# New orders for every engine's queue in a token-block and convolution kernel, and one more square on VectorE

## The chip, the core and the metric

The kernel runs on one core of a Trainium2 chip. The metric is the device time of one execution in microseconds (us), as the median of several runs. A core has five engines that work side by side, each with its own queue, in order: TensorE (PE: matrix products and transposes, results in PSUM; PEld is its weight load), VectorE (DVE), ScalarE (ACT), GpSimd (POOL), and SyncE (SP), which here issues DMAs. An instruction waits, at the head of its engine's queue, for semaphores of the engines whose results or buffers it needs; what stands behind it waits too.

## The reference

Input x is (4, 128, 128, 128) in float32: four images, 128 channels, 128 x 128 pixels. Two layers follow each other, each on a group-normalised input and added to it:

```python
# layer 0, for each token (pixel) t of 128 channels; it is applied to the image and to
# its transpose and added: for a token-wise block that is twice the same
t = _ln(t, ln0_g, ln0_b)
y1 = _ln(t, ln1_g, ln1_b)
t = t + einsum('btc,oc->bto', sigmoid(y1) * y1, W_out)
y2 = _ln(t, ln2_g, ln2_b)
wht = einsum('btc,oc->bto', y2, W_whiten)
k = square(relu(einsum('btc,hc->bth', wht, W_key)))        # 512 wide
kv = einsum('bth,ch->btc', k, W_value)
r = sigmoid(einsum('btc,oc->bto', wht, W_recep))
t = t + r * kv
...
x = x + _L0_conv_ref(_gn(x), ...)
x = x + _L1_conv_ref(_gn(x), ...)   # 3 x 3 convolution, bias, times a squeeze-and-excite gate
```

## The kernel before

**Tiling.** Tokens go in 64 pairs, 16 to an image; a pair is two halves of 512 tokens, each of four 128-token pieces. In an operation's name the first digit after the letters is the half or the norm's number, a second digit is the half or the key block; the number after the colon says which pair or convolution block is meant, relative to the slot, or counted from somewhere, according to the list. The convolution works on 32 blocks of 16 rows (8 to an image), where each group of four output rows comes from six products (c0 to c5) in place of twelve, after Winograd; each product is three matrix products (L875 to L877) of shifted columns. Its inputs v0 to v5 and outputs y0 to y3 are sums on VectorE.

**One token pair, in order of data.** ACT lays the group norm on the input (u), TensorE transposes it (Tu, L659), VectorE takes statistics (bn, L690), POOL makes the norm's factors (nb, L707 to L725, with the power at L718; in the first two pairs VectorE does the rest and POOL the power, names sa and pw), ACT applies it (t, L666), POOL multiplies and shifts (g at L742, b at L746). Then the second norm (bn1, nb1, ACT's z, L666), a transpose (Tz), ACT's silu (L757), TensorE's product (att, L763), VectorE's sum (T, L767), the third statistics (bn2, nb2). The third norm's factors go through HBM to be spread over the partitions: VectorE turns them (rc, L775), SP writes four short rows (W, L781) and reads them back as R (L786, twice 256 KB), while TensorE transposes t (tt). VectorE multiplies the two (cp, L799). From that come four key products for each half (pk, L810), ACT's relu (re, L814), the square (sq, on ACT at L820, or on VectorE at L824, where it reads pk again), the gate's product (pr, L828) with ACT's tanh (th, L832), four value products that add up in one bank (kv, L837), and VectorE's and POOL's sums back into the block (S L847, q L853, x L857), whose statistics (bx, L863) the second layer's norm uses. Around this, fetch and in0/in1 (L998, L1004) read the next image and take its statistics.

**Order.** A manual schedule: every engine runs its instructions in the order in which the lists name them. FILL (L37) starts pairs 0 to 5 and the first slots; FIRST (L66) is repeated for slots 6 to 16, where no convolution is there yet; HANDOVER (L80) leads to the second image, with the setup of the first image's convolution; ORDER (L25) is repeated for 21 slots (23 to 30, 39 to 46, 55 to 59), each with a token pair at several ages and half a convolution block; BOUND (L143) leads twice from one image to the next; END (L210) has the last four pairs and all the convolution of the last image. In these, `*` is the next step of a convolution's setup (statistics mv, pm, pv, root rs, scaled weights, gate; L555 to L632), `+` one of the next image's input norm, `load` reads a block. After the last token pairs, END is convolution alone.

**Buffers.** PSUM's eight banks: two for ut, two for the transposes and att (tr), two for keys (h), one for the convolution and one for kv. Until pair 18 every third key product goes to the convolution's bank (key_bank, L801). A bank comes free when its last reader ends. In SBUF there are six relu outputs h, two u, two z, four t, three R and two r.

**Squares.** FIRST_SQUARES (L270) says for the pairs of the first image which key blocks of each half are squared on ACT (A) or VectorE (D); SQUARES has A everywhere for the other three images.

Of the kernel before, what the change touches and what calls it, by code (L numbers as in the profile page):

```python
# [25 lines left out]
    u1:0 Tu1:0 u0:0 x11:3 Tz10:1 Tu0:0 bn01:0 bn00:0 z11:1 bx1:3 v1:1 pr0:2 Tz11:1 q2:1  # L26
    silu0:1 p2:1 re00:2 sq00:2 y2:1 ca:1 att0:1 silu1:1 c0:1 pk01:2 nb0:0 d8:1 kv00:2 T0:1
    y0:1 th0:2 t1:0 bn20:1 v3:1 tt1:2 g1:0 re01:2 in0:0 c1:1 cp1:2 e1:1 att1:1 pk02:2 c3:1
    T1:1 bn21:1 pk10:2 c5:1 b1:0 y3:1 re02:2 S1:2 t0:0 nb2:1 e3:1 pk03:2 v2:1 g0:0 b0:0
    re10:2 c2:1 in1:0 a:1 pk12:2 sq01:2 sq10:2 v0a:1 sq02:2 re03:2 sq03:2 re12:2 b:1 kv01:2  # L30
    kv02:2 rc:1 pk13:2 re13:2 v4:1 pk11:2 kv03:2 sq12:2 c4:0 bn11:0 v5a:0 tt0:1 bn10:0 v0b:1
    pr1:2 q0:2 c:0 d:0 re11:2 sq11:2 S0:1 sq13:2 kv10:2 v5b:0 kv11:2 th1:2 kv12:2 kv13:2
    nb1:0 W:1 y1:0 R0:1 z10:0 q:0 cp0:1 pk00:1 R1:1 x10:2 p:0 bx0:2 q1:2
# [4 lines left out]
    fetch:16 u1:0 u0:0 Tu1:0 bn01:0 u0:1 Tu0:0 u1:1 bn00:0 sa0:0 in1:16 pw0:0 in0:16  # L38
    fetch:17 nb0:0 t1:0 t0:0 Tu0:1 g1:0 bn00:1 b1:0 u1:2 Tu1:1 in1:17 g0:0 u0:2 in0:17
    bn11:0 fetch:18 b0:0 bn01:1 sa0:1 bn10:0 pw0:1 sa1:0 nb0:1 pw1:0 in1:18 t0:1 in0:18  # L40
    nb1:0 fetch:19 t1:1 Tu1:2 g0:1 bn01:2 b0:1 z10:0 Tu0:2 bn00:2 g1:1 z11:0 Tz10:0 b1:1
    in0:19 silu0:0 Tz11:0 bn10:1 nb0:2 u0:3 att0:0 in1:19 silu1:0 bn11:1 fetch:20 u1:3
    att1:0 sa1:1 T0:0 bn20:0 pw1:1 t0:2 T1:0 t1:2 bn21:0 g0:2 sa2:0 Tu0:3 nb1:1 pw2:0 Tu1:3
    in1:20 u1:4 in0:20 z10:1 g1:2 bn00:3 fetch:21 z11:1 bn01:3 nb2:0 b0:2 Tz10:1 rc:0 nb0:3
    W:0 silu0:1 Tz11:1 att0:1 silu1:1 in1:21 bn10:2 R0:0 att1:1 in0:21 b1:2 t0:3 T0:1
    fetch:22 T1:1 tt0:0 t1:3 g0:3 bn11:2 R1:0 tt1:0 Tu1:4 nb1:2 cp0:0 u0:4 bn20:1 u0:5 Tu0:4
    pk02:0 in1:22 S1:0 u1:5 bn01:4 pk00:0 re02:0 pk01:0 re00:0 g1:3 cp1:0 pk03:0 z10:2
    sq00:0 b1:3 bn00:4 pk11:0 re01:0 b0:3 re03:0 pr0:0 in0:22 z11:2 bn21:1 fetch:23 kv00:0
    nb0:4 pk10:0 S0:0 sq01:0 bn10:3 Tz10:2 re11:0 kv01:0 silu0:2 sa2:1 pk12:0 re10:0 bn11:3
    att0:2 sq02:0 pw2:1 sq03:0 kv02:0 T0:2 th0:0 nb2:1 nb1:3 Tz11:2 t1:4 rc:1 kv03:0 sq10:0  # L50
    W:1 pk13:0 q0:0 silu1:2 Tu1:5 in0:23 re12:0 att1:2 bn20:2 t0:4 R0:1 pr1:0 g1:4 bn01:5
    kv10:0 sq11:0 R1:1 x10:0 T1:2 Tu0:5 sq12:0 kv11:0 z10:3 bn00:5 tt1:1 tt0:1 nb0:5 kv12:0
    th1:0 cp0:1 re13:0 pr0:1 sq13:0 cp1:1 pk03:1 z11:3 S1:1 pk00:1 bn21:2 th0:1 kv13:0 g0:4
    S0:1 re00:1 Tz11:3 bx0:0 pk01:1 re03:1 b1:4 sq00:1 silu1:3 pk02:1 b0:4 bn11:4 re01:1
    Tz10:3 att1:3 re02:1 nb2:2 bn10:4 silu0:3 pk12:1 q1:0 pk10:1 re12:1 T1:3 att0:3 sq03:1
    bn21:3 sq01:1 kv00:1 nb1:4 re10:1 pk11:1 sq02:1 rc:2 sq10:1 W:2 pk13:1 re11:1 T0:3
    kv01:1 sq11:1 bn20:3 t1:5 kv02:1 x11:0 R0:2 kv03:1 sq12:1 nb2:3 tt0:2 q0:1 re13:1 R1:2
    pr1:1 bx1:0 t0:5 kv10:1 S0:2 kv11:1 sq13:1 kv12:1 x10:1 z10:4 cp0:2 tt1:2 pk01:2 g0:5
    S1:2 th1:1 pk00:2 cp1:2 re01:2 g1:5 pk03:2 re00:2 rc:3 kv13:1 sq00:2 re03:2 in1:23
    pk02:2 q1:1 pk10:2 bx0:1 x11:1 kv00:2 Tz10:4 bx1:1  # L60
# [6 lines left out]
    u1:0 u0:0 Tu1:0 pk11:4 re02:4 pr0:4 z11:2 Tu0:0 in1:0 re10:4 silu0:2 Tz11:2 sq01:4  # L67
    bn01:0 W:3 att0:2 b1:1 sq10:4 bn00:0 R0:3 T0:2 th0:4 silu1:2 re11:4 kv01:4 b0:1 pk12:4
    sq03:4 tt0:3 bn10:1 sq02:4 pk13:4 sq11:4 cp0:3 re12:4 pr1:4 att1:2 th1:4 kv02:4 re13:4
    kv03:4 nb0:0 bn11:1 bn20:2 T1:2 S0:3 pk01:3 pk00:3 pk03:3 bn21:2 tt1:3 t0:0 q0:4 kv10:4  # L70
    nb1:1 sq12:4 kv11:4 re01:3 re00:3 sq13:4 in0:0 nb2:2 S1:3 kv12:4 sq00:3 kv13:4 R1:3
    x10:4 cp1:3 pk02:3 rc:2 q1:4 bx0:4 t1:0 x11:4 g1:0 z10:1 bx1:4 pk10:3 kv00:3 Tz10:1 g0:0
    re03:3
# [7 lines left out]
    load load load fetch:32 sq01:13 W:14 z11:15 re02:13 Tz11:15 R0:14 silu0:15 kv01:13 u1:17  # L81
    att0:15 R1:14 silu1:15 b0:16 pk11:13 T0:15 re10:13 att1:15 bn20:15 b1:16 u0:17 pk13:13
    re11:13 T1:15 Tu1:17 * bn21:15 tt0:14 re13:13 pr1:13 sq03:13 sq10:13 nb2:15 pr0:13
    sq02:13 bn01:17 u1:18 Tu0:17 pk12:13 bn00:17 sq11:13 kv02:13 th0:13 bn10:16 nb0:17
    sq13:13 tt1:14 kv03:13 th1:13 cp0:14 re12:13 q0:13 pk00:14 u0:18 bn11:16 kv10:13 sq12:13
    re00:14 pk01:14 cp1:14 x10:13 t1:17 S1:14 kv11:13 sq00:14 pk03:14 nb1:16 S0:14 t0:17
    Tu1:18 kv12:13 re01:14 pk12:14 bn01:18 re03:14 Tu0:18 u0:19 pk02:14 bn00:18 g0:17
    kv13:13 z10:16 rc:15 W:15 g1:17 tt0:15 q1:13 pk10:14 sq03:14 S0:15 sq01:14 nb0:18
    kv00:14 * re12:14 kv01:14 * re02:14 R0:15 * re10:14 pr0:14 bx0:13 sq02:14 R1:15 sq10:14
    pk11:14 sq12:14 Tz10:16 th0:14 b0:17 kv02:14 t1:18 kv03:14 x11:13 cp0:15 pk13:14 re11:14  # L90
    bn10:17 b1:17 t0:18 pk00:15 q0:14 pr1:14 bn11:17 sq11:14 x10:14 Tu0:19 * tt1:15 kv10:14
    * * nb1:17 th1:14 * kv11:14 re00:15 * kv12:14 cp1:15 re13:14 bn00:19 silu0:16 pk02:15
    sq13:14 sq00:15 re02:15 kv13:14 g0:18 S1:15 u1:19 pr1:15 q1:14 z11:16 b0:18 att0:16
    bx0:14 pk01:15 x11:14 z10:17 Tu1:19 Tz11:16 g1:18 bn01:19 pk03:15 th1:15 silu1:16
    kv00:15 T0:16 nb0:19 re01:15 bn20:16 pr0:15 z11:17 att1:16 bn10:18 re03:15 in1:32
    Tz11:17 pk10:15 sq01:15 T1:16 b1:18 sq03:15 bn21:16 Tz10:17 kv01:15 re10:15 nb2:16
    sq02:15 sq10:15 pk11:15 silu1:17 bx1:14 kv02:15 th0:15 kv03:15 silu0:17 t0:19 q0:15
    att0:17 rc:16 x10:15 bn11:18 W:16 pk12:15 re11:15 bx1:13 tt0:16 nb1:18 sq11:15 pk13:15
    T0:17 u0:20 bx0:15 t1:19 R0:16 Tu0:20 bn20:17 kv10:15 kv11:15 R1:16 re12:15 S0:16
    re13:15 att1:17 bn00:20 g0:19 sq12:15 sq13:15 kv12:15 g1:19 * kv13:15 cp0:16 u1:20 *  # L100
    b1:19 u1:21 Tu1:20 q1:15 pk01:16 z10:18 bn01:20 x11:15 pk00:16 nb0:20 re01:16 bx1:15
    Tz10:18 pr0:16 re00:16 T1:17 sq00:16 * tt1:16 silu0:18 bn21:17 * th0:16 att0:18 sq01:16
# [164 lines left out]
"""  # L267

SQUARES = ("AAAA", "AAAA")
FIRST_SQUARES = ("DAAA", "DAAA")  # L270

ON_GPSIMD = set()
END_ON_GPSIMD = {"p2", "q2"}
# [912 lines left out]
```

## Time and profile before

| what | us |
|---|---|
| median of three runs (1869.79 to 1872.17) | 1870.11 |
| the profiled execution | 1872.87 |
| its span in the profile | 1871.1 |
| TensorE busy | 1806.3 |
| VectorE busy | 1348.0 |
| ACT busy | 1269.8 |
| POOL busy | 1164.7 |
| ACT's squares (L820), 480 | 286.5 |
| VectorE's squares (L824), 32 | 23.6 |

The profiled execution took 1.8 us more than its span, and 2.8 us more than the median of the runs. A page has one line for every group of instructions: its line in the code, engine, operation, what it writes and reads, number, then busy time and mean duration in ns, then the time that the engine stood idle before them, with what ended it. In a timeline, a line gives start, duration and the instruction, and in brackets the idle time before it. One record of TensorE may last beyond the start of the next, since products are pipelined.

### The profile page before, as it was taken

Reading aid. Unit: us, or ns where it says so; the run is one execution under the profiler, and the core shown is the slowest. Engines: PE = TensorE matmul, PEld = TensorE weight load, DVE = VectorE, ACT = ScalarE, POOL = GpSimd, SP = SyncE. Lnnn points to the kernel's source line nnn. Section 1 sums busy time; section 2 is a strip of 40 time slices with the busy share of each in tenths; the row PEclk is TensorE's granted clock in tenths of the full one; section 3 lists DMA queues with packets and bytes.
Section 4 is the critical chain, followed back from the end, with each engine's and each line's share of the span. In section 5 each row is a group of like instructions: output and inputs, shape, how many; then the busy total and the mean of one; then the engine's idle time right before and its main releaser. Section 6 shows DMA issues by size and latency. Waiting matters only on the chain.

```text
span 1871.1 us, 21825 instructions
## 1 busy us (share of the span) xinstructions
PE 1806.3 (97%) x6096; PEld 942.6 (50%) x6096; DVE 1348.0 (72%) x3336; ACT 1269.8 (68%) x2493; POOL 1164.7 (62%) x1915
## 2 busy tenths in 40 slices
PE   3799999999999999999999999999999999999999
PEld 2555555555545555455455455455455555554443
DVE  6767766677677677777757677777766667676987
ACT  2889899898666776777667777677766777753000
POOL 2878888887366666886556666788555667641211
PEclk9899999999999999999999999999999999999999
DMA  5211112221212212222112212211201111111112
GB/s 219 89 46 57 46 49 96 73 71 58 71 59 85 91 68 103 84 87 96 42 68 91 77 50 77 75 63 68 81 12 68 68 57 68 50 39 45 52 68 90
DMA packets 46072, 133.57 MB, mean 71 GB/s; under 512 B 8679, under 2 KB 15102, under 8 KB 38014
## 3 DMA queue, kind: packets, MB, share of 16 engines
q1 hardware_dynamic: 45504, 131.77, 20.5%
q8 instruction: 49, 0.80, 0.2%
q14 instruction: 73, 0.60, 0.1%
q10 hardware_dynamic: 446, 0.40, 0.1%
HBM read 97.14 MB, written 35.00 MB: 71 GB/s over the span
## 4 chain that ended last, share of the span: by engine, by line
PE 84%; DVE 5%; POOL 5%; DMA 3%; ACT 2%; issue 1%; SPq 0%; DVEq 0%; POOLq 0%
PE kv L837 21%; PE pk L810 21%; PE m L875 8%; PE m L877 8%; PE m L876 8%; PE pr L828 5%; PE att L763 5%; PE tt L659 3%; PE ut L659 3%; PE z1t L659 3%; DMA x<-in_x 1%; POOL rs L718 1%; DMA R<-rd 1%; DVE st L690 1%; ACT t L666 1%
## 5 line engine op out<-in xcount | busy, mean ns | idle before, releaser
L810 PE MATMUL pk<-y,wk_s 128*128 128x512 f32 x1024 | 503.3, 594 | 1.6 <-ACT h L814 0.9
L837 PE MATMUL kv<-h,wv 128*128 128x512 f32 x1024 | 492.7, 593 | 0.0
L814 ACT ACTIVATE h<-pk,kbias 128x512 f32<-128x512 f32 x512 | 349.3, 687 | 188.1 <-PE pk L810 178.3
L857 POOL TENSOR_TENSOR x<-x,r 128x512 f32<-128x512 f32 x128 | 166.7, 1302 | 202.4 <-DVE r L853 193.2
L837 PEld LDWEIGHTS kv<-h,wv 128*128 128x128 f32 x1024 | 187.1, 190 | 201.9 <-issue 177.2
L820 ACT ACTIVATE h<-h 128x512 f32<-128x512 f32 x480 | 286.5, 629 | 3.4
L810 PEld LDWEIGHTS pk<-y,wk_s 128*128 128x128 f32 x1024 | 183.0, 191 | 185.2 <-issue 148.0
L666 ACT ACTIVATE t<-ut,nb,rs 128x128 f32<-128x128 f32 x512 | 191.4, 466 | 90.6 <-POOL nb L725 82.7
L690 DVE BATCH_NORM_STATS2 st<-t 128x6 f32<-128x128 f32 x1024 | 219.0, 278 | 30.5 <-POOL t L746 28.7
L666 ACT ACTIVATE z<-t,nb,rs 128x128 f32<-128x128 f32 x512 | 209.5, 489 | 17.5 <-POOL nb L725 17.1
L718 POOL TENSOR_TENSOR rs<-rs,nhalf 128x8 f32<-128x8 f32 x128 | 215.4, 1682 | 6.0 <-DVE rs L711 6.0
L742 POOL TENSOR_TENSOR t<-t,g 128x512 f32<-128x512 f32 x128 | 163.8, 1285 | 74.7 <-ACT t L666 74.3
L875 PE MATMUL m<-v,u 128*128 128x512 f32 x384 | 198.5, 598 | 10.4 <-DVE v L899 5.0
L877 PE MATMUL m<-v,u 128*128 128x508 f32 x384 | 195.7, 591 | 0.0
L876 PE MATMUL m<-v,u 128*128 128x508 f32 x384 | 195.5, 591 | 0.0
L746 POOL TENSOR_TENSOR t<-t,b 128x512 f32<-128x512 f32 x128 | 166.0, 1304 | 5.6
L853 DVE SCALAR_TENSOR_TENSOR r<-r,kv 128x512 f32<-128x512 f32 x128 | 87.0, 680 | 86.2 <-PE kv L837 83.4
L763 PEld LDWEIGHTS att<-wo,y 128*128 128x128 f32 x1024 | 131.9, 196 | 31.5 <-issue 22.4
L767 DVE TENSOR_TENSOR t<-att,t 128x512 f32<-128x512 f32 x128 | 87.7, 685 | 78.3 <-PE att L763 77.8
L690 DVE BATCH_NORM_STATS2 st<-ut 128x6 f32<-128x128 f32 x512 | 112.3, 283 | 40.4 <-PE ut L659 39.8
L763 PE MATMUL att<-wo,y 128*128 128x128 f32 x1024 | 138.0, 280 | 0.8 <-DVE t L767 0.4
L828 PE MATMUL pr<-y,wr_s 128*128 128x512 f32 x256 | 130.7, 594 | 0.9 <-DVE h L824 0.7
(164 smaller groups left out, 2491.2 us busy)
## 6 DMA issues: line engine op xcount, KB each, us to landing
R<-rd SPq DMA_DIRECT2D x128, 256.0 KB
x<-in_x SPq DMA_DIRECT2D x31, 1024.0 KB
out<-x SPq DMA_DIRECT2D x31, 1024.0 KB
xs<-in_x SPq DMA_DIRECT2D x48, 512.0 KB
rd<-rrow SPq DMA_DIRECT2D x256, 1.0 KB
u<-raw SPq DMA_DIRECT2D x18, 192.0 KB
raw<-u SPq DMA_DIRECT2D x6, 192.0 KB
x<-in_x SPq DMA_DIRECT2D x2, 512.0 KB
```

The costliest lines, as they stand in the source:

```text
L666: nc.scalar.activation(dst[:, s, :], src[:, s, :], AF.Identity, bias=nb[:, i : i + 1], scale=rs[:, i : i + 1],)
L690: nc.vector.bn_stats(st[:, h * SUB + s, :], src[:, s, :])
L718: nc.gpsimd.tensor_tensor(rs, rs, nhalf, ALU.pow)
L763: nc.tensor.matmul(att[:, ts(s, P)], y[:, ts(s, P)], wo, start=True, stop=True)
L810: nc.tensor.matmul(pk, wk_s[:, ts(j, P)], S["y2", g, h], start=True, stop=True)
L814: nc.scalar.activation(k, S["pk", g, h, j], AF.Relu, bias=kbias[:, j : j + 1])
L820: nc.scalar.activation(k, k, AF.Square)
L828: nc.tensor.matmul(pr, wr_s, S["y2", g, h], start=True, stop=True)
L837: nc.tensor.matmul(S["kv", g, h], wv[:, j, :], S.pop(("h", g, h, j)), start=(j == 0), stop=(j == NH - 1))
L875: nc.tensor.matmul(pc, u[:, 1], v, start=True, stop=False)
L876: nc.tensor.matmul(pc[:, :, 1:W], u[:, 0], v[:, :, 0 : W - 1], start=False, stop=False)
L877: nc.tensor.matmul(pc[:, :, 0 : W - 1], u[:, 2], v[:, :, 1:W], start=False, stop=True)
```

## The change

All six lists are replaced. Each new list has the same operations as the old one, so that no operation is added or taken away; what changes is the order on each engine's queue, among them the loads and the writes and reads of R on SP's. How the new lists were made isn't in the code. The functions stay as they are, and so do the numbers of slots. In FIRST_SQUARES one more letter is D: in the 16 pairs of the first image, the second key block of the second half (sq11) is squared on VectorE. The heads of the long lists are shown, ORDER and FIRST whole:

```diff
--- before.py
+++ after.py
 ORDER = """
-    u1:0 Tu1:0 u0:0 x11:3 Tz10:1 Tu0:0 bn01:0 bn00:0 z11:1 bx1:3 v1:1 pr0:2 Tz11:1 q2:1
-    silu0:1 p2:1 re00:2 sq00:2 y2:1 ca:1 att0:1 silu1:1 c0:1 pk01:2 nb0:0 d8:1 kv00:2 T0:1
-    y0:1 th0:2 t1:0 bn20:1 v3:1 tt1:2 g1:0 re01:2 in0:0 c1:1 cp1:2 e1:1 att1:1 pk02:2 c3:1
-    T1:1 bn21:1 pk10:2 c5:1 b1:0 y3:1 re02:2 S1:2 t0:0 nb2:1 e3:1 pk03:2 v2:1 g0:0 b0:0
-    re10:2 c2:1 in1:0 a:1 pk12:2 sq01:2 sq10:2 v0a:1 sq02:2 re03:2 sq03:2 re12:2 b:1 kv01:2
-    kv02:2 rc:1 pk13:2 re13:2 v4:1 pk11:2 kv03:2 sq12:2 c4:0 bn11:0 v5a:0 tt0:1 bn10:0 v0b:1
-    pr1:2 q0:2 c:0 d:0 re11:2 sq11:2 S0:1 sq13:2 kv10:2 v5b:0 kv11:2 th1:2 kv12:2 kv13:2
-    nb1:0 W:1 y1:0 R0:1 z10:0 q:0 cp0:1 pk00:1 R1:1 x10:2 p:0 bx0:2 q1:2
+    u1:0 p:1 kv00:3 u0:0 z10:1 sq02:3 Tu0:0 kv01:3 Tu1:0 kv02:3 re03:3 d:1 bn00:0 rc:2
+    Tz10:1 bn01:0 c2:2 in1:0 re12:3 z11:1 pk11:3 nb0:0 sq03:3 Tz11:1 a:2 silu0:1 sq10:3 W:2
+    sq12:3 re11:3 kv03:3 silu1:1 t0:0 R0:2 sq11:3 q2:1 q:1 tt0:2 t1:0 pk13:3 pr1:3 v3:1 c3:1
+    q0:3 re13:3 th1:3 att1:1 v4:1 b:2 g0:0 v1:1 e3:1 v5a:0 kv10:3 S0:2 cp0:2 att0:1 b0:0
+    g1:0 kv11:3 sq13:3 b1:0 T1:1 pk02:2 T0:1 y1:1 re02:2 y2:1 ca:1 kv12:3 bn10:0 bn11:0
+    v5b:0 x10:3 pk01:2 R1:2 bn20:1 re01:2 kv13:3 tt1:2 pr0:2 v0a:1 cp1:2 nb1:0 c0:1 sq01:2
+    v0b:1 q1:3 y0:1 th0:2 c1:1 pk00:2 bn21:1 pk10:2 bx0:3 x11:3 c5:1 e1:1 d8:1 re00:2 sq00:2
+    bx1:3 re10:2 in0:0 c4:0 pk12:2 c:0 nb2:1 y3:1 S1:2 p2:0 pk03:2 v2:1
 """
 
 
...
 FILL = """
-    fetch:16 u1:0 u0:0 Tu1:0 bn01:0 u0:1 Tu0:0 u1:1 bn00:0 sa0:0 in1:16 pw0:0 in0:16
-    fetch:17 nb0:0 t1:0 t0:0 Tu0:1 g1:0 bn00:1 b1:0 u1:2 Tu1:1 in1:17 g0:0 u0:2 in0:17
-    bn11:0 fetch:18 b0:0 bn01:1 sa0:1 bn10:0 pw0:1 sa1:0 nb0:1 pw1:0 in1:18 t0:1 in0:18
-    nb1:0 fetch:19 t1:1 Tu1:2 g0:1 bn01:2 b0:1 z10:0 Tu0:2 bn00:2 g1:1 z11:0 Tz10:0 b1:1
-    in0:19 silu0:0 Tz11:0 bn10:1 nb0:2 u0:3 att0:0 in1:19 silu1:0 bn11:1 fetch:20 u1:3
-    att1:0 sa1:1 T0:0 bn20:0 pw1:1 t0:2 T1:0 t1:2 bn21:0 g0:2 sa2:0 Tu0:3 nb1:1 pw2:0 Tu1:3
-    in1:20 u1:4 in0:20 z10:1 g1:2 bn00:3 fetch:21 z11:1 bn01:3 nb2:0 b0:2 Tz10:1 rc:0 nb0:3
-    W:0 silu0:1 Tz11:1 att0:1 silu1:1 in1:21 bn10:2 R0:0 att1:1 in0:21 b1:2 t0:3 T0:1
-    fetch:22 T1:1 tt0:0 t1:3 g0:3 bn11:2 R1:0 tt1:0 Tu1:4 nb1:2 cp0:0 u0:4 bn20:1 u0:5 Tu0:4
-    pk02:0 in1:22 S1:0 u1:5 bn01:4 pk00:0 re02:0 pk01:0 re00:0 g1:3 cp1:0 pk03:0 z10:2
-    sq00:0 b1:3 bn00:4 pk11:0 re01:0 b0:3 re03:0 pr0:0 in0:22 z11:2 bn21:1 fetch:23 kv00:0
-    nb0:4 pk10:0 S0:0 sq01:0 bn10:3 Tz10:2 re11:0 kv01:0 silu0:2 sa2:1 pk12:0 re10:0 bn11:3
...
+    fetch:16 u0:0 u1:0 Tu0:0 bn00:0 u0:1 Tu1:0 u1:1 bn01:0 sa0:0 in0:16 pw0:0 in1:16
+    fetch:17 nb0:0 t0:0 t1:0 Tu0:1 g0:0 bn00:1 u1:2 Tu1:1 g1:0 in0:17 u0:2 b1:0 bn01:1
+    in1:17 b0:0 bn11:0 fetch:18 sa0:1 bn10:0 pw0:1 sa1:0 nb0:1 pw1:0 in1:18 t0:1 in0:18
+    fetch:19 nb1:0 t1:1 Tu1:2 g0:1 bn01:2 b0:1 z10:0 Tu0:2 g1:1 bn10:1 z11:0 Tz10:0 bn00:2
+    b1:1 silu0:0 Tz11:0 bn11:1 att0:0 silu1:0 sa1:1 u1:3 att1:0 in0:19 u0:3 pw1:1 in1:19
+    T0:0 fetch:20 nb0:2 nb1:1 T1:0 z11:1 bn20:0 Tz11:1 bn21:0 silu1:1 sa2:0 t1:2 att1:1
+    in0:20 pw2:0 in1:20 t0:2 fetch:21 Tu1:3 g1:2 T1:1 bn01:3 u1:4 Tu0:3 g0:2 z10:1 bn00:3
+    nb2:0 b1:2 rc:0 Tz10:1 W:0 b0:2 bn11:2 silu0:1 bn21:1 nb0:3 u0:4 att0:1 bn10:2 R0:0
+    tt0:0 in1:21 R1:0 in0:21 T0:1 nb1:2 t1:3 S0:0 fetch:22 tt1:0 bn20:1 t0:3 Tu1:4 cp0:0
+    sa2:1 pk01:0 u1:5 S1:0 g0:3 z11:2 cp1:0 pk00:0 bn01:4 b0:3 pk03:0 re00:0 in1:22 Tz11:2
+    re01:0 g1:3 Tu0:4 sq00:0 silu1:2 pk10:0 bn00:4 pw2:1 z10:2 att1:2 bn10:3 kv00:0 re03:0
+    b1:3 T1:2 Tz10:2 sq01:0 pr0:0 bn21:2 re10:0 nb0:4 pk02:0 silu0:2 bn11:3 kv01:0 re02:0
...
 FIRST = """
-    u1:0 u0:0 Tu1:0 pk11:4 re02:4 pr0:4 z11:2 Tu0:0 in1:0 re10:4 silu0:2 Tz11:2 sq01:4
-    bn01:0 W:3 att0:2 b1:1 sq10:4 bn00:0 R0:3 T0:2 th0:4 silu1:2 re11:4 kv01:4 b0:1 pk12:4
-    sq03:4 tt0:3 bn10:1 sq02:4 pk13:4 sq11:4 cp0:3 re12:4 pr1:4 att1:2 th1:4 kv02:4 re13:4
-    kv03:4 nb0:0 bn11:1 bn20:2 T1:2 S0:3 pk01:3 pk00:3 pk03:3 bn21:2 tt1:3 t0:0 q0:4 kv10:4
-    nb1:1 sq12:4 kv11:4 re01:3 re00:3 sq13:4 in0:0 nb2:2 S1:3 kv12:4 sq00:3 kv13:4 R1:3
-    x10:4 cp1:3 pk02:3 rc:2 q1:4 bx0:4 t1:0 x11:4 g1:0 z10:1 bx1:4 pk10:3 kv00:3 Tz10:1 g0:0
-    re03:3
+    u0:0 u1:0 re03:4 Tu1:0 bn10:1 th0:4 z11:2 re02:4 R0:3 Tu0:0 kv00:4 pk12:4 bn01:0 silu0:2
+    pk11:4 bn00:0 R1:3 att0:2 in1:0 sq02:4 kv01:4 T0:2 re12:4 re11:4 pk13:4 Tz11:2 sq03:4
+    b1:1 bn11:1 in0:0 sq12:4 nb0:0 pk10:4 sq11:4 tt0:3 kv02:4 re13:4 bn20:2 cp0:3 S0:3
+    silu1:2 kv03:4 pr1:4 re10:4 t1:0 sq13:4 t0:0 tt1:3 th1:4 q0:4 sq10:4 pk01:3 nb1:1 att1:2
+    x10:4 S1:3 pk00:3 re01:3 T1:2 kv10:4 bn21:2 g0:0 kv11:4 sq01:3 kv12:4 bx0:4 re00:3
+    kv13:4 q1:4 sq00:3 nb2:2 x11:4 cp1:3 rc:2 bx1:4 b0:0 pk03:3 z10:1 pr0:3 W:2 pk02:3 g1:0
+    Tz10:1
 """
 FIRST_SLOTS = 17
...
 HANDOVER = """
-    load load load fetch:32 sq01:13 W:14 z11:15 re02:13 Tz11:15 R0:14 silu0:15 kv01:13 u1:17
-    att0:15 R1:14 silu1:15 b0:16 pk11:13 T0:15 re10:13 att1:15 bn20:15 b1:16 u0:17 pk13:13
-    re11:13 T1:15 Tu1:17 * bn21:15 tt0:14 re13:13 pr1:13 sq03:13 sq10:13 nb2:15 pr0:13
...
+    load load load z11:15 u0:17 u1:17 re03:13 Tu1:17 Tz11:15 th0:13 bn01:17 Tu0:17 silu0:15
+    pr1:13 bn00:17 b1:16 sq03:13 att0:15 fetch:32 silu1:15 bn10:16 kv00:13 nb0:17 re02:13
+    R0:14 att1:15 sq02:13 bn11:16 u0:18 pk13:13 R1:14 T1:15 th1:13 pk10:13 bn21:15 re13:13
...
 BOUND = """
-    p2:-3 q2:-3 fetch:0 v3:-3 x11:-4 * u0:-1 u1:-1 load Tu0:-1 z11:-2 Tu1:-1 re00:-3 Tz10:-2
-    pk01:-3 v1:-3 * bn00:-1 bn01:-1 v0a:-3 v4:-3 c3:-3 + * sq00:-3 Tz11:-2 silu0:-2 re01:-3
-    att0:-2 silu1:-2 v2:-3 in0:0 nb0:-1 e3:-3 att1:-2 t0:-1 + T0:-2 g0:-1 c1:-3 + e1:-3
-    tt1:-3 b0:-1 bn20:-2 T1:-2 + cp1:-3 t1:-1 pk03:-3 re03:-3 + in1:0 sq03:-3 bn21:-2
-    bn10:-1 c2:-3 + g1:-1 pk10:-3 + kv00:-3 pk02:-3 u0:0 a:-3 Tu0:0 b1:-1 b:-3 u0:1 p:-2
-    fetch:1 bn11:-1 sq01:-3 v0b:-3 v5a:-3 re02:-3 bn00:0 c4:-3 c:-3 u1:0 re10:-3 Tu1:0
...
+    z10:-2 u0:-1 Tz10:-2 rc:-3 u1:-1 Tu0:-1 kv00:-4 z11:-2 Tu1:-1 q2:-3 Tz11:-2 v3:-3
+    kv01:-4 load silu0:-2 W:-3 bn00:-1 silu1:-2 att0:-2 re03:-4 bn01:-1 p:-3 nb0:-1 re12:-4
+    sq02:-4 + att1:-2 c3:-3 q:-3 sq12:-4 R0:-3 * T0:-2 kv02:-4 T1:-2 sq03:-4 v1:-3 + e3:-3
+    v4:-3 fetch:0 + kv03:-4 pk13:-4 t0:-1 g0:-1 tt0:-3 t1:-1 sq10:-4 q0:-4 re13:-4 + cp0:-3
+    R1:-3 bn21:-2 c1:-3 + pk11:-4 b0:-1 + g1:-1 re11:-4 bn10:-1 bn20:-2 kv10:-4 b1:-1 +
+    in1:0 x10:-4 bn11:-1 tt1:-3 pk00:-3 sq13:-4 S0:-3 in0:0 e1:-3 pr1:-4 nb1:-1 re00:-3
...
 END = """
-    u1:3 Tu1:3 u0:3 d8:-5 z11:4 Tu0:3 bn00:3 Tz10:4 bn01:3 pk03:5 Tz11:4 silu0:4 x11:6
-    re00:5 silu1:4 att0:4 pr0:5 y2:-5 att1:4 re03:5 nb0:3 T0:4 bn20:4 c0:-5 sq00:5 th0:5
-    kv00:5 tt1:5 t0:3 t1:3 pk01:5 T1:4 bn21:4 u1:2 re01:5 nb2:4 ca:-5 sq01:5 g0:3 p:-4 p2:-4
-    y0:-5 cp1:5 pk02:5 u0:2 c5:-5 sq03:5 bx1:6 re02:5 S1:5 g1:3 b1:3 rc:4 y3:-5 b0:3 bn11:3
-    bn10:3 kv01:5 Tu1:2 sq02:5 pk10:5 nb1:3 bn01:2 re10:5 Tu0:2 sq10:5 pk11:5 q:-4 v1:-4 W:4
-    pk13:5 kv02:5 tt0:4 re11:5 pr1:5 re13:5 kv03:5 th1:5 c1:-4 z10:3 bn00:2 z11:3 v2:-4 R0:4
-    Tz10:3 q0:5 cp0:4 q2:-4 pk12:5 silu0:3 nb0:2 pk00:4 re12:5 x10:5 e1:-4 v5a:-4 v3:-4 S0:4
-    R1:4 v0a:-4 t1:2 t0:2 v0b:-4 g1:2 kv10:5 att0:3 Tz11:3 T0:3 pr0:4 g0:2 sq11:5 silu1:3
-    re00:4 load c3:-4 sq13:5 sq12:5 kv11:5 u1:1 att1:3 b0:2 bn10:2 sq00:4 pk02:4 b1:2 kv12:5
-    bn11:2 tt1:4 kv13:5 nb1:2 T1:3 e3:-4 Tu1:1 c2:-4 u0:1 th0:4 re02:4 S1:4 bn21:3 bn20:3
-    u0:0 q1:5 a:-4 z10:2 b:-4 pk01:4 cp1:4 Tu0:1 pk03:4 kv00:4 bx0:5 re01:4 nb2:3 pk10:4
...
+    u1:3 u0:3 Tu1:3 z11:4 kv00:6 Tz11:4 d:-5 re03:6 sq03:6 bn01:3 rc:5 z10:4 Tu0:3 bn00:3
+    nb0:3 silu1:4 c2:-5 sq02:6 re12:6 att1:4 t1:3 kv01:6 Tz10:4 T1:4 t0:3 kv02:6 kv03:6 a:-5
+    b:-5 g0:3 W:5 y2:-5 g1:3 b1:3 y1:-5 ca:-5 pk13:6 R1:5 silu0:4 d8:-5 b0:3 c0:-5 att0:4
+    y0:-5 pk11:6 bn21:4 u1:2 tt0:5 re11:6 T0:4 bn20:4 c5:-5 re13:6 nb2:4 q0:6 R0:5 cp0:5
+    Tu1:2 bn10:3 y3:-5 x10:6 bn11:3 sq13:6 tt1:5 pr1:6 sq12:6 cp1:5 nb1:3 sq10:6 pk02:5
+    bx0:6 sq11:6 S0:5 th1:6 u0:2 re02:5 p:-4 load rc:4 bn01:2 q2:-4 kv10:6 kv11:6 pk00:5
+    sq02:5 pr0:5 W:4 Tu0:2 re00:5 pk01:5 sq00:5 kv12:6 th0:5 p2:-4 pk13:5 bn00:2 tt0:4
+    kv13:6 re01:5 z10:3 S0:4 pk10:5 re13:5 q1:6 q:-4 sq01:5 z11:3 nb0:2 pk03:5 x11:6 kv00:5
+    kv01:5 re03:5 R0:4 re10:5 kv02:5 R1:4 sq10:5 cp0:4 sq03:5 sq13:5 pk12:5 pk11:5 S1:5
+    tt1:4 kv03:5 re12:5 re11:5 sq11:5 Tz10:3 pk02:4 t0:2 pr1:5 sq12:5 q0:5 re02:4 t1:2 th1:5
+    kv10:5 cp1:4 kv11:5 g0:2 u0:1 v3:-4 u1:1 S1:4 kv12:5 pk00:4 b0:2 kv13:5 q1:5 sq02:4
+    Tz11:3 re00:4 Tu0:1 Tu1:1 g1:2 b1:2 v1:-4 x11:5 silu0:3 pk03:4 pk01:4 c3:-4 silu1:3
+    re01:4 sq01:4 re03:4 bn01:1 x10:5 att1:3 e3:-4 bn00:1 bn10:2 v4:-4 nb0:1 v0a:-4 bn11:2
+    nb1:2 att0:3 T1:3 pk11:4 pr0:4 u0:0 sq00:4 T0:3 re11:4 c1:-4 v2:-4 pk10:4 t0:1 t1:1
...
 SQUARES = ("AAAA", "AAAA")
-FIRST_SQUARES = ("DAAA", "DAAA")
+FIRST_SQUARES = ("DAAA", "DDAA")
```

## Prediction before the run

> **What bounds the kernel now.** I read the busy list first, then the forty slices, the chain of waits, TensorE's waits, a table of stretches, and last the timeline around each place where TensorE stood still. The page:
>
> ```profile
> span 1871.1 us, 21825 instructions
> PE 1806.3 (97%) x6096; PEld 942.6 (50%) x6096; DVE 1348.0 (72%) x3336; ACT 1269.8 (68%) x2493; POOL 1164.7 (62%) x1915
> PE   3799999999999999999999999999999999999999
> PE 84%; DVE 5%; POOL 5%; DMA 3%; ACT 2%; issue 1%; SPq 0%; DVEq 0%; POOLq 0%
> ```
>
> TensorE bounds it everywhere but in the first two slices (94 us). Busy time can't say how closely it is packed, since a record (594 ns) is longer than the distance between two starts (430 ns). I therefore count starts: a 128x512 product, two records, takes 0.859 us; four transposes 0.437; one attention half (eight records) 0.891; one convolution product (three such pairs) 2.566. A token pair is 8 key, 8 value and 2 gate products, 6 groups of transposes and 2 attention halves: 18 x 0.859 + 6 x 0.437 + 2 x 0.891 = 19.87 us. 64 pairs and 192 convolution products are 1271.7 + 492.7 = 1764.4 us, and all work of TensorE, setup included, comes to about 1780. So some 85 us of the span are gaps: 32.7 before 50 us, 17.6 from 50 to 100, a fixed tail of 4.3, and about 30 spread thinly over the 1,750 us between. New orders can only win from these. The waits of TensorE and VectorE, with total, count and longest:
>
> ```profile
> PE ut L659 <- ACT t L666: 17.8, 8, 7.4
> PE m L875 <- DVE v L899: 5.0, 5, 1.6
> PE pr L828 <- DVE h L824: 0.7, 1, 0.7
> DVE y L799 <- DMA R<-rd: 23.1, 16, 4.7
> ```
>
> The first is mostly the start. The last doesn't stop TensorE each time, but in places does: there the order gave the round trip of R through HBM too little other work. Where the start, one slot of FIRST and the middle and end stand (start:end, length, PE, PEld, DVE, ACT, POOL busy, clock):
>
> ```profile
> 50.00:100.00 50.00, 43.25 (x167) 27.29 (x168) 39.32 (x134) 43.23 (x95) 44.60 (x74) 0.90 0.25 74
> 150.00:200.00 50.00, 50.00 (x182) 26.96 (x181) 34.72 (x92) 45.86 (x95) 40.23 (x74) 1.00 0.19 54
> 700.00:750.00 50.00, 47.97 (x174) 25.36 (x172) 38.78 (x97) 33.18 (x65) 28.52 (x50) 1.00 0.27 97
> 1700.00:1750.00 50.00, 44.96 (x111) 19.58 (x110) 40.54 (x73) 11.44 (x21) 10.93 (x8) 1.00 0.11 37
> ```
>
> The second line is FIRST: ACT is 92% busy, yet TensorE has no gap; by the timeline one slot runs from 189.80 to 209.67, which is 19.87, the packed sum. In the start POOL is the fullest of the side engines (44.6 of 50). The dated stalls:
>
> ```profile
> 736.75 1.13 PE L810 MATMUL pk<-y,wk_s 128*128 128x512 f32 x2 [0.44 <-DVE y L799]
> 741.64 1.10 PE L875 MATMUL m<-v,u 128*128 128x512 f32 x2 [1.59 <-DVE v L899]
> 1190.59 1.10 PE L875 MATMUL m<-v,u 128*128 128x512 f32 x2 [1.59 <-DVE v L899]
> 1726.21 0.38 PE L558 MATMUL pm<-mv,gmat 128*128 128x1 f32 x2 [1.90 <-DVE mv L555]
> 1741.15 1.13 PE L875 MATMUL m<-v,u 128*128 128x512 f32 x2 [1.17 <-DVE v L899]
> ```
>
> They lie where one list gives way to another. By bracketed idle times: HANDOVER and its neighbourhood (345 to 530 us) 0.68 + 0.90 + 0.30 + 0.90 + 2.07 = 4.85; first BOUND (700 to 900) 0.44 + 1.59 + 1.51 + 0.77 = 4.31; second BOUND (1190 to 1241) 1.59 + 0.53 + 0.38 = 2.50; END (1721 to 1742) 0.41 + 1.90 + 0.48 + 0.37 + 0.72 + 1.17 = 5.05.
>
> **What the Trainium skill says.** "Perfetto Trace Analysis", Identifying the Most-Contended Engine, calls matmul busy time a poor measure because of the pipelining; the trace agrees (97% busy with the gaps above). "SBUF — State Buffer", SBUF: two separate sides, says that a VectorE operation with two SBUF inputs and a GpSimd operation lock each other out for a whole instruction. The trace agrees: at 739.01 a sum of two SBUF tiles took 1.76 us beside a POOL operation, against 0.69 for its neighbours. The square on VectorE has one input in PSUM, and its 32 records lie between 709 and 752 ns: not stretched. "PSUM — Partial Sum Buffer", PSUM bank collisions raise a hardware error, has every bank guarded by semaphores; so a square on VectorE, which reads pk again, keeps its bank until it ends. The 0.7 us line above is such a wait. "DMA: Bandwidth & Descriptors", Anatomy of one DMA, gives about 2.0 us fixed plus bytes over 436 GB/s, an estimate of 2.6 us for R; the trace has 3.44 (732.54 to 735.98) with the row's write before it, 8.4 us from rc's end to cp there (6.6 in the start), and the trace decides.
>
> **The change, part by part.** No operation is added or dropped; positions change on all five engines' queues, and 16 squares (sq11, the second one of the pair's second half, in pairs 0 to 15) go from ACT to VectorE.
>
> Squares: 16 x 0.60 = 9.6 us leave ACT and 16 x 0.74 = 11.8 come to VectorE. Both engines have idle time in FIRST, and TensorE is packed, so the value is 0. Without that cover: in the new FIRST list kv13 must end, then q1 (0.60) runs, then sq00 (0.74), before pk02 may take the bank. That is 0.20 + 0.60 + 0.74 + 0.04 = 1.58 us, and TensorE has pk03 and pr0 = 1.72 in between. The spare is 0.14 us; in the old list the corresponding one is about 0.8. Taken: 0; bounds 0 and +3 (0.3 us in each of 11 slots).
>
> FILL: up to pw2:0, which ended at 66.04 on POOL, both lists do nearly the same. Then the new POOL queue has g1, g0, b1, b0 of pair 2 (4 x 1.27) and two norm blocks of 3.65 (rows 74.96 to 78.60): nb1:2 ends at about 66.0 + 5.1 + 7.3 = 78.4. On ACT z11:2 (1.6) waits for it and now stands ahead of re00 and re01 (0.69 each), which the old list ran first. pk10:0 reuses the bank that re01 frees: 78.4 + 1.6 + 1.4 = 81.4, or 82.0 with what else may come between. Ahead of it the list has 13.6 us of TensorE work, so the work runs at an offset of 67.8 to 68.4, against 65.7 at the first pk (76.29, with 10.6 us listed ahead) and 66.5 by 100 us in the trace. On VectorE cp0:0 has 2.4 us more listed ahead (34.0 against 31.6), which agrees: 74.2 becomes 76.6. Taken: +1.8; bounds 0 (the packed POOL sets the pace anyway) and +3.
>
> FIRST: 0, as TensorE has no gap to give.
>
> HANDOVER: of 4.85 us I can date each stall but can't date the new list's, since setup steps and loads lie between. About half of that is taken back: −2; bounds −5 and +4.
>
> ORDER: 21 slots with almost no gap. Its convolution products now come three and three in the two halves of the slot instead of four and two; rc and cp0 stay 9 us of TensorE work apart (before 10 and 7). −0.5; bounds −2 and +2.
>
> BOUND, twice: c3 now comes first, its VectorE inputs stand earlier, and the distance from rc to cp0 goes to 9 and more everywhere, above the 8.4 of the round trip. The 0.44 and both 1.59 should go; the wait on ut for POOL's norm too. Late next is the image's setup chain ahead of c3, with a spare of about 1.6 us by the rows, less when POOL and VectorE meet (1.1 us each). −3.0 of 4.31 and −1.5 of 2.50; bounds together −6.8 and +2.
>
> END: the last image's setup chain (mv, pm, rs, scaling, v) starts some 5 us of TensorE work earlier in the list (pm at 1627 instead of 1632 of work done), with more products of the image before behind it. But rc and cp0 of pair 62 are only 3 us apart, and VectorE stands behind that cp for up to 8.4 − 3 = 5.4 us. −2.5 of 5.05; bounds −5 and +3.
>
> Tail 4.3 us: unchanged. Sum: 1.8 − 2 − 0.5 − 3.0 − 1.5 − 2.5 = −7.7 us. The profiled run took 1872.87 (span 1871.1 and 1.8 around it), so 1865.2 for such a run; it lay 2.8 above the median, 1870.1, which becomes 1862.4, said as 1862.5.
>
> **Rivals.** (a) As summed: 1862.5, spread 1857 to 1866. (b) Gaps are only shifted: packed lists make new collisions between VectorE and POOL for each stall they remove, and the start keeps its loss: +1.8 − 3 = about −1, 1869. For it: the stalls are single events of 0.4 to 2 us, each as long as one stretched instruction. Against it: several have a named cause (R, order of v) that the lists move. (c) Nearly all goes: −16.7 us of dated stalls, and the start loses nothing, 1854. For it: every stretch between is packed today. Against: the setup chain's latency remains. (d) Slower: sq00 comes late in FIRST. VectorE's squares today waited 3.6 us in five cases for ACT's relu, at the longest 1.3; were that to recur each slot, pk02 would wait 1.3 − 0.14 = 1.16 us, in 11 slots 12.8, less the 7.7 won: +5.1, 1875. It decides from 0.14 us on, and turns the sign once a slot loses 0.7. For it: ACT is 92% busy there and sets when relu is done. Against: ACT gets 0.6 us lighter, and nothing stretches the square. That the change doesn't do what it says isn't a case: all durations are measured rows, but whether the lists fit them is (b).
>
> **How the numbers follow.** Two thousandths, 3.7 us, is about what a measurement can tell from no change. (a) 0.50, (b) 0.18, (c) 0.15, (d) 0.17. Faster takes (a) less its weak end, (c), and a few of (b): 0.67. Same: 0.17. Slower: (d) less its mild end, and (b)'s bad end: 0.16. The range 1852 to 1874 takes in (a), (b), (c) and the mild part of (d); the likeliest case alone is 1857 to 1866.
>
> **What would show it.** First key product at about 77 instead of 76.3, and pk10 near 82; slots of FIRST still 19.87 from value product to value product, without a line of pk waiting for VectorE's h; no v or y wait in 730 to 745 and near 1190; R's 23.1 us of VectorE idle well down, with a long one left in END; pm's wait near 1726 below 1 us. A FIRST slot above 20.0 would make me wrong on the squares; new stalls of over 3 us in ORDER or HANDOVER, wrong on the lists.

## The result and the profile after

The changed kernel takes 1941.79 us (median of four runs, 1940.33 to 1943.78) where the kernel before takes 1870.28: a ratio of 1.0381, with a 95% interval of 1.0363 to 1.0399. It is 71.5 us slower. The forecast was 1862.5, and its range ended at 1874. The profiled execution took 1942.5, with a span of 1940.7.

The page, with the waits of TensorE and VectorE (engine, line, what was waited for, total, count, longest). The changed kernel's lines from L268 on have numbers higher by one, so L876 is the L875 of before; other runs have the one or the other.

```profile
span 1940.7 us, 21885 instructions
PE 1825.0 (94%) x6096; PEld 947.6 (49%) x6096; DVE 1402.4 (72%) x3352; ACT 1261.9 (65%) x2477; POOL 1169.6 (60%) x1915
PE   3899999999899889999988988999999999999999
PE 77%; DVE 9%; DMA 8%; POOL 2%; issue 1%; ACT 1%; SPq 0%; DVEq 0%; POOLq 0%
```

```profile
PE m L876 <- DVE v L900: 48.5, 8, 7.3
PE pk L811 <- ACT r L833: 6.7, 4, 3.2
PE pk L811 <- DVE h L825: 2.9, 2, 2.8
...
DVE st L1005 <- DMA xs<-in_x: 62.5, 17, 7.1
DVE y L800 <- DMA R<-rd: 20.8, 9, 5.4
```

The row of slices has 8s where there were 9s before: slices 11, 14 and 15, and 21, 22, 24 and 25, in the two stretches of ORDER in which the next image is still read. The chain of waits now has 8% of DMA, where it had 3%. One line holds the loss: eight waits of a convolution product for VectorE's v, 48.5 us, which were five with 5.0 in all. VectorE itself waited 62.5 us for xs, the next image's input, 47.3 of them in eight places just ahead of those eight waits. The stretches (start:end, length, PE, PEld, DVE, ACT, POOL, clock, DMA share, GB/s) show FIRST as full as before, ORDER not:

```profile
150.00:200.00 50.00, 50.00 (x185) 26.86 (x183) 35.24 (x93) 44.59 (x90) 40.24 (x72) 1.00 0.14 43
700.00:750.00 50.00, 43.99 (x151) 23.10 (x150) 31.80 (x68) 30.85 (x62) 27.77 (x43) 0.93 0.20 69
1050.00:1100.00 50.00, 44.14 (x145) 22.51 (x144) 33.39 (x74) 32.31 (x66) 25.78 (x46) 0.93 0.24 85
```

One of the eight, in selected lines of the changed kernel's timeline (start, duration, instruction, idle time before it):

```profile
1051.38 0.67 DVE L974 TENSOR_TENSOR x<-m,e 128x512 f32<-128x512 f32 x1
1052.12 0.34 SPq L987 DMA_DIRECT2D out<-x  x1
1054.80 0.20 DVE L776 STREAM_TRANSPOSE rrow<-four 128x32 f32<-128x32 f32 x1
1055.98 0.33 SPq L359 DMA_DIRECT2D x<-in_x  x1
1056.36 0.43 SPq L999 DMA_DIRECT2D xs<-in_x  x1
1056.84 1.41 SPq L782 DMA_DIRECT2D rd<-rrow  x4
1061.91 0.69 DVE L1005 BATCH_NORM_STATS2 st<-xs 128x6 f32<-128x512 f32 x1 [5.74 <-DMA xs<-in_x]
1062.58 0.82 SPq L787 DMA_DIRECT2D R<-rd  x2
...
1066.72 2.07 PE L876 MATMUL m<-v,u 128*128 128x512 f32 x2 [5.86 <-DVE v L900]
1071.97 1.12 PE L764 MATMUL att<-wo,y 128*128 128x128 f32 x8
```

From the top: y3, the block's last row, lets the 1 MB store go (1052.12). The next slot is odd and begins with the load of a new block. It isn't issued until 1055.98, 3.9 us after the store, because it waits for that store to land: SP waited for such landings at the load 20 times, 71.1 us in all, in the kernel before 9 times, 26.1 us (the two lines below). Behind the load in SP's queue stand the fetch of xs and W, whose input was there from about 1055. VectorE stands at in1 until xs has landed, and behind in1 stand q2, q and v3, for which TensorE waits 5.86 us. The same turn in the kernel before has W and R ahead of the load and the fetch:

```profile
SPq L359 <- DMA out<-x: 71.1, 20, 4.6
SPq L358 <- DMA out<-x: 26.1, 9, 3.9
...
559.87 0.34 SPq L986 DMA_DIRECT2D out<-x  x1
561.13 2.13 SPq L781 DMA_DIRECT2D rd<-rrow  x4
564.61 0.82 SPq L786 DMA_DIRECT2D R<-rd  x2
565.52 0.37 SPq L358 DMA_DIRECT2D x<-in_x  x1
565.94 0.43 SPq L998 DMA_DIRECT2D xs<-in_x  x1
```

R is late on top: W goes out 1.8 us after its input is there, and R's two reads 5.7 us after W. In the kernel before W goes out at once, and the reads follow 3.5 to 4.9 us after it in ORDER's slots with a store just ahead, and about 2.3 in the others (561.13 to 564.61, and 589.86 to 592.18). And the product that was waited for runs from 1066.72 to 1071.97, 5.25 us where it takes 2.57, at a granted clock of 0.50. In the eight cases it took 4.1 to 5.3 us, together some 18 more than eight times 2.57. These 18 and the 48.5 of waiting make 66 of the 71.5.

Two pages of the Trainium skill bear on this. "DMA: Bandwidth & Descriptors", Anatomy of one DMA, says that DMA engines don't wait on semaphores: the wait happens on the issuing sequencer before dispatch. So a load that waits for a buffer holds up whatever is behind it in SP's list; the trace agrees (load, fetch and W go out within 0.9 us as soon as the load may). "TensorE: Matmul & The Clock Gate", What's actually happening, says that TensorE falls to half its clock after an idle window of about 3.4 us; the trace agrees for the eight gaps of 5.9 to 7.3 us, with the granted clock at 0.93 over these stretches and records of 2.07 us against 1.10. The last section has shorter gaps, which fit it less well.

In the order of SP's list the difference is plain (words of ORDER's 113 counted from 0). Before: store (y3 is word 48), W, R0, R1 (words 101, 103, 108), then, at the next slot, load and fetch; in1 and in0 come at words 60 and 36 of that slot. After: store (y3 word 108), load, fetch, then W and R (27, 33, 75), with in1 at word 17 and in0 at 103. There is one buffer for xs, freed by in0 late in a slot and wanted by in1 early in the next.

### The profile page after: what moved, and what is told of

Read it like the earlier page. It is cut to its first block, busy times and chain, and to the rows that moved or that the text cites. A ratio compares the mean times of both kernels' runs of the same rounds, so it can differ in the third digit from the quotient of the medians.

```text
span 1940.7 us, 21885 instructions
## 1 busy us (share of the span) xinstructions
PE 1825.0 (94%) x6096; PEld 947.6 (49%) x6096; DVE 1402.4 (72%) x3352; ACT 1261.9 (65%) x2477; POOL 1169.6 (60%) x1915
## 4 chain that ended last, share of the span: by engine, by line
PE 77%; DVE 9%; DMA 8%; POOL 2%; issue 1%; ACT 1%; SPq 0%; DVEq 0%; POOLq 0%
PE pk L811 19%; PE kv L838 19%; PE m L876 8%; PE m L877 7%; PE m L878 7%; PE att L764 5%; PE pr L829 5%; DMA xs<-in_x 3%; DMA out<-x 3%; PE tt L660 2%; PE z1t L660 2%; PE ut L660 2%; DMA x<-in_x 2%; DVE st L691 2%; DVE st L1005 1%
## 5 line engine op out<-in xcount | busy, mean ns | idle before, releaser
L811 PE MATMUL pk<-y,wk_s 128*128 128x512 f32 x1024 | 511.6, 597 | 10.3 <-ACT r L833 6.7
L838 PE MATMUL kv<-h,wv 128*128 128x512 f32 x1024 | 508.6, 594 | 0.0
L821 ACT ACTIVATE h<-h 128x512 f32<-128x512 f32 x464 | 282.1, 630 | 3.0
L876 PE MATMUL m<-v,u 128*128 128x512 f32 x384 | 205.8, 618 | 53.9 <-DVE v L900 48.5
L838 PEld LDWEIGHTS kv<-h,wv 128*128 128x128 f32 x1024 | 178.5, 191 | 144.7 <-issue 135.5
L858 POOL TENSOR_TENSOR x<-x,r 128x512 f32<-128x512 f32 x128 | 175.6, 1373 | 107.2 <-DVE r L854 106.9
L743 POOL TENSOR_TENSOR t<-t,g 128x512 f32<-128x512 f32 x128 | 169.6, 1327 | 95.2 <-ACT t L667 95.1
L877 PE MATMUL m<-v,u 128*128 128x508 f32 x384 | 202.1, 609 | 0.0
L878 PE MATMUL m<-v,u 128*128 128x508 f32 x384 | 199.2, 601 | 0.0
L708 POOL TENSOR_TENSOR rs<-st 128x8 f32<-128x8 f32 x124 | 37.9, 306 | 238.2 <-DVE st L691 238.2
L747 POOL TENSOR_TENSOR t<-t,b 128x512 f32<-128x512 f32 x128 | 177.3, 1387 | 6.4
```

The lines of the kernel that those rows point to most:

```text
L747: nc.gpsimd.tensor_tensor(t, t, over(b0), ALU.add)
L811: nc.tensor.matmul(pk, wk_s[:, ts(j, P)], S["y2", g, h], start=True, stop=True)
L821: nc.scalar.activation(k, k, AF.Square)
L838: nc.tensor.matmul(S["kv", g, h], wv[:, j, :], S.pop(("h", g, h, j)), start=(j == 0), stop=(j == NH - 1))
L876: nc.tensor.matmul(pc, u[:, 1], v, start=True, stop=False)
L877: nc.tensor.matmul(pc[:, :, 1:W], u[:, 0], v[:, :, 0 : W - 1], start=False, stop=False)
```

## The experiments

Each ratio is to runs of the kernel before that were taken together with the run in question (medians of 1869.61 to 1870.70).

| run | what is different | median, us | ratio to before, 95% interval |
|---|---|---|---|
| changed kernel | | 1941.79 | 1.0381 (1.0363 to 1.0399) |
| e4_squares_back | squares of sq11 on ACT again | 1941.08 | 1.0382 (1.0367 to 1.0398) |
| e2_fetch_first | fetch ahead of the load | 1908.12 | 1.0204 (1.0184 to 1.0224) |
| e5_load_mid | load in the slot's middle | 1904.40 | 1.0187 (1.0157 to 1.0218) |
| e7_handover_too | e5 and two HANDOVER edits | 1897.61 | 1.0146 (1.0129 to 1.0163) |
| e8_and_squares_back | e7 and squares on ACT again | 1897.76 | 1.0147 (1.0122 to 1.0171) |
| e1_in1_later | in1 in the slot's middle | 1894.68 | 1.0134 (1.0117 to 1.0151) |
| e11_in1_and_load | e1 and e5 | 1876.95 | 1.0032 (1.0021 to 1.0043) |
| e14_fetch_load_mid | fetch and load behind R1, in1 and in0 last | 1874.76 | 1.0020 (1.0011 to 1.0029) |
| e15_hand_fetch_load | e14 and the HANDOVER edits | 1870.04 | 0.9995 (0.9987 to 1.0003) |
| e16_loads_later | e15 and three moves more | 1863.34 | 0.9969 (0.9960 to 0.9978) |
| e3_before_in_moved | old lists, in1 early and in0 late | 1880.38 | 1.0056 (1.0035 to 1.0076) |
| e17_before_chain | e3 and the load ahead of W | 1915.36 | 1.0241 (1.0220 to 1.0262) |

**The place of in1, in the new list and in the old.**

```diff
 ORDER (changed kernel, e1)
-    Tz10:1 bn01:0 c2:2 in1:0 re12:3
+    Tz10:1 bn01:0 c2:2 re12:3
...
+    g1:0 kv11:3 sq13:3 b1:0 in1:0 T1:1
...
 ORDER (kernel before, e3; both words taken from their old places)
+    ... bn00:0 in1:0 z11:1 ... q:0 cp0:1 pk00:1 R1:1 x10:2 p:0 in0:0 bx0:2 q1:2
```

> The changed kernel with one word moved in ORDER: the second half's input statistics (in1:0) go from 17 words into the slot to about the middle, behind b1:0. Theory A (the one buffer of the next image's input is freed by in0 late in one slot and wanted by in1 early in the next, with a 1 MB block load ahead of its fetch on SP's queue in odd slots, so VectorE and then TensorE stand still in eight slots): the eight waits of VectorE for xs of 5.4 to 7.1 us in ORDER go, and with them about 68 us, to 1870 to 1880. Rival B (the ORDER list is late on VectorE anyway, the xs wait only shows it first): the waits for v stay as waits for something else, and the time stays above 1920.

> The kernel before, with its old lists, but in ORDER in1:0 moved to the slot's start (behind bn00:0) and in0:0 to its end (behind p:0), as the new list has them. Theory A: eight long waits of VectorE for xs come up in odd slots and cost what they cost in the changed kernel, 5 to 9 us each, 1910 to 1945. Rival B (the new list as a whole): no more than 10 us, below 1880.

Moving one word (e1) brought 47 of the 71.5 us, and the eight waits for xs in ORDER went. But the forecast of 1870 to 1880 was missed by 15 us. In their place came, eight times, a wait of 1.4 to 2.8 us of att for VectorE, which stood at cp for R. The timeline of e1:

```profile
506.38 0.34 SPq L987 DMA_DIRECT2D out<-x  x1
511.05 0.33 SPq L359 DMA_DIRECT2D x<-in_x  x1
511.44 0.43 SPq L999 DMA_DIRECT2D xs<-in_x  x1
511.91 1.43 SPq L782 DMA_DIRECT2D rd<-rrow  x4
517.55 0.82 SPq L787 DMA_DIRECT2D R<-rd  x2
520.71 0.69 DVE L800 TENSOR_TENSOR y<-tt,R 128x512 f32<-128x512 f32 x1 [3.95 <-DMA R<-rd]
521.54 1.13 PE L764 MATMUL att<-wo,y 128*128 128x128 f32 x8 [1.72 <-DVE y L800]
```

SP's queue is the same: rc ended at 509.64, W went out at 511.91, and R reached VectorE 11.1 us after rc, 2.7 more than the 8.4 of the prediction. The changed kernel itself has a milder case, the last stretch of ORDER, where nothing is fetched any more: loads stand ahead of W three times, and TensorE waits once, 1.86 us (1482.42).

In the old lists the same two places of in1 and in0 (e3) cost only 10.7 us, where I had expected 40 or more: there W and R are ahead of the load, and the longest wait for xs is 3.0. So the places of in1 and in0 alone weren't the cause, which left the order on SP to be tried.

**The order on SP.** e2 puts the fetch ahead of the load; e5 moves the load behind R1, in the middle of the slot.

```diff
 def slot(s, order):                     (e5)
-    if s % 2 and s + 1 >= NP and len(blocks) < B * NBLK:
-        load_block(len(blocks))
...
     for n, (op, k) in enumerate(order):
+        if n == 76 and s % 2 and s + 1 >= NP and len(blocks) < B * NBLK:
+            load_block(len(blocks))
```

> The changed kernel with the fetch of the next image's input issued ahead of the block load in odd slots, all lists as they are. Theory A with the block load as the thing in the way: xs lands before in1 or at most 1.5 us late, as it does in even slots today; at least 50 of the 71 us go: 1870 to 1892. Rival C (the time from in0 to in1 is too short for the 512 KB by itself): the waits shrink by less than half, above 1905.

> The changed kernel, all lists as they are; in odd slots the block load is issued in the middle of the slot, behind R1, instead of at its start. Theory A2 (the chain store of the last block, landing, load, fetch, W, R on SP's one queue: the new list puts y3 and so the store at the slot's end, so the load waits for it at the head of the queue and what stands behind it, the fetch and W, is late): the fetch goes out right behind in0 and W right behind rc; the eight waits for xs fall to 1 us or less, R isn't late either, 1868 to 1880. Rival A1 (only the distance from in0 to in1 is too short): no better than the fetch put first, 1895 to 1910. Rival E (the data of the load beside R and xs, wherever it stands): some 2 us left in each of eight slots, 1885 to 1895.

Each brought about half (34 and 37 us), and both missed their theory. e2 landed where its rival C was to land (above 1905), though not for that rival's reason: the waits for xs shrank from 5.4 to 7.1 us to 1.7 to 3.3, by more than half. e5 landed in the range of its rival A1, no better than the fetch put first. In its timeline the fetch now goes out 0.4 us after the store, and W at once behind rc, yet xs is 2.1 us late. From the fetch's issue to in1 it took 5.8 us, with the store's 1 MB in flight, where in the eight waits in FIRST, with no store or load about, it took 3.3 to 4.2:

```profile
567.43 0.34 SPq L987 DMA_DIRECT2D out<-x  x1
567.81 0.43 SPq L999 DMA_DIRECT2D xs<-in_x  x1
573.61 0.69 DVE L1005 BATCH_NORM_STATS2 st<-xs 128x6 f32<-128x512 f32 x1 [2.13 <-DMA xs<-in_x]
...
577.23 1.77 DVE L900 SCALAR_TENSOR_TENSOR v<-p,mg,q 128x512 f32<-128x512 f32 x1
578.93 1.62 DVE L932 TENSOR_TENSOR v<-x 128x384 f32<-128x384 f32 x1
580.48 1.35 DVE L938 TENSOR_TENSOR v<-x,x 128x128 f32<-128x128 f32 x1
582.49 0.68 DVE L800 TENSOR_TENSOR y<-tt,R 128x512 f32<-128x512 f32 x1
583.31 1.13 PE L764 MATMUL att<-wo,y 128*128 128x128 f32 x8 [2.56 <-DVE y L800]
```

The three operations between run at 1.77, 1.62 and 1.35 us, where in e1 they took 0.75, 0.56 and 0.28: 3.15 us more. I read that as the meeting with POOL that the prediction described: in e5 POOL's products for t run beside them (577.19 to 581.68), in e1 they start only after them (517.49). No run took POOL away. The two delays come to 5.3 us, of which 2.56 reach att. What either would cost alone wasn't tried.

**Both paths.** e1 leaves R late, and e2 and e5 leave xs late. Together:

```diff
 def slot(s, order):       (e14; middle = 76 in ORDER's slots; taken from the slot's start)
+        if n == middle:
+            for g in now[:1]:
+                fetch_stats(g)
+            if s % 2 and s + 1 >= NP and len(blocks) < B * NBLK:
+                load_block(len(blocks))
...
 ORDER                                   (in1 and in0 taken from their old places)
+    bx0:3 in1:0 ... pk03:2 v2:1 in0:0
```

> Both partial repairs together: in1:0 in the middle of ORDER's slot, and the block load in the slot's middle. Theory A3 (two separate paths from one cause: the store, load and fetch at the slot's turn delay xs for in1, and they delay W and so R for cp; either alone stops VectorE ahead of v and cp): neither xs nor R is late by more than 1.5 us, TensorE has no stall of over 1 us in ORDER's odd slots, 1872 to 1880. Rival G (VectorE's own work in the odd slots is too long between rc and cp, whatever the DMAs do): att still waits 2 us or more for VectorE's y in each odd slot, 1888 to 1905.

> In ORDER's slots the fetch and, behind it, the block load are issued in the middle, behind R1, and the two statistics in1 and in0 come at the slot's end: on SP the order is then store, W, R, fetch, load, as it was in the kernel before in its own phase. Theory A3: no wait for xs, R late by at most what the store's own data cost, 1868 to 1878. Rival G: as before, above 1888.

Both fell inside their ranges, and the timeline marks no idle time of TensorE at all in e14's two reading stretches (450 to 750 and 900 to 1200 us). There SP's timeline has W and R right behind the store again, as in the kernel before, W 2.3 us ahead of R; only the fetch is now ahead of the load:

```profile
566.57 0.34 SPq L987 DMA_DIRECT2D out<-x  x1
569.85 1.29 SPq L782 DMA_DIRECT2D rd<-rrow  x4
572.16 0.82 SPq L787 DMA_DIRECT2D R<-rd  x2
573.03 0.43 SPq L999 DMA_DIRECT2D xs<-in_x  x1
573.50 0.44 SPq L359 DMA_DIRECT2D x<-in_x  x1
```

So 67 of the 71.5 us come from the turn of the odd slots. The last test puts the load ahead of W in the old lists, too. It isn't quite the changed kernel's turn, since the fetch stays behind R:

```diff
 def slot(s, order):                     (kernel before with e3's two moves, e17)
-        if s % 2 and s + 1 >= NP and len(blocks) < B * NBLK:
+        if s in (NP - 1, ORDER_FROM, 39, 55):
             load_block(len(blocks))
...
     for n, (op, k) in enumerate(order):
+        if (op, k) == ("W", 1) and s > ORDER_FROM and s % 2 == 0 and s not in (30, 46):
+            load_block(len(blocks))
```

> The kernel before with its old lists, the two statistics moved as in the run on them (in1:0 at the slot's start, in0:0 at its end), and in addition the block load of an odd slot issued in the slot before, just ahead of W:1, so that on SP the order is store, load, W, R, fetch, as the new lists have it. Theory A3: W and R wait behind the load, R comes 4 to 6 us late in some eight slots, and TensorE stands still for most of it: 1905 to 1940. Rival H (the new list's own order on VectorE is what costs): below 1890, as with the statistics alone (1880).

It is 35 us slower than e3, inside its range, and 46 slower than the kernel before. The old list, too, loses 3.1 to 3.8 us of TensorE for each of the eight loads that stand ahead of W:

```profile
621.37 0.34 SPq L986 DMA_DIRECT2D out<-x  x1
625.56 0.33 SPq L358 DMA_DIRECT2D x<-in_x  x1
625.95 1.33 SPq L781 DMA_DIRECT2D rd<-rrow  x4
630.96 0.82 SPq L786 DMA_DIRECT2D R<-rd  x2
634.36 0.69 DVE L799 TENSOR_TENSOR y<-tt,R 128x512 f32<-128x512 f32 x1 [5.86 <-DMA R<-rd]
635.11 1.97 PE L810 MATMUL pk<-y,wk_s 128*128 128x512 f32 x2 [3.80 <-DVE y L799]
```

**The squares.**

```diff
-FIRST_SQUARES = ("DAAA", "DDAA")
+FIRST_SQUARES = ("DAAA", "DAAA")
```

> The changed kernel with the 16 squares of sq11 back on ACT, all else as it is. Theory A: the squares have next to no part in the loss; 1938 to 1943, at most 3 us faster, which is the one wait of a key product for a square on VectorE at 356.85 us. Rival D (a bank held by the square): over 8 us faster, below 1934.

> The same as the kernel with both HANDOVER edits, but the 16 squares of sq11 back on ACT. If the square is hidden, as I took it to be: within 2 us of it. If its bank decides in FIRST: 2 to 5 us faster than it. If ACT, at 92% there, had needed the relief: slower by 2 us or more.

0.7 us of 1941 and 0.15 us of 1897, both within the spread of the runs: by the times the move of the squares shows neither cost nor gain. The traces show one small price: a slot of FIRST that took 20.30 us takes 19.93 with the squares back on ACT (e4). In the old lists the move can't be priced: with it alone (e9) the kernel before deadlocks, and there is no time for it.

**HANDOVER, and a version that beats both.**

```diff
 HANDOVER (e7, e15; and a yield of its own behind the weights' DMAs in conv_setup)
-    load load load z11:15 ... att0:15 fetch:32 silu1:15 ... u0:18 pk13:13
+    fetch:32 load load load z11:15 ... att0:15 silu1:15 ... u0:18 * pk13:13
 HANDOVER and BOUND (e16)
-    fetch:32 load load load z11:15
+    fetch:32 z11:15 ... R1:14 load load load T1:15 ... nb2:15 u0:18 u1:18
-    e3:-2 x11:-4 u0:2 kv02:-3 ... th1:-3 nb1:0
+    e3:-2 x11:-4 kv02:-3 ... th1:-3 u0:2 nb1:0
```

> The kernel with the load in the middle of the slot, and in HANDOVER two things: fetch:32 ahead of the three block loads instead of behind them, and the DMA of the convolution's weights issued one setup step of its own earlier (behind u0:18), so that ACT's first scaling of them doesn't wait. Theory A2 carried over to HANDOVER: the wait of 2.8 us of a key product for VectorE's square at 356 us and that of 3.2 us for ACT's tanh at 394 us go, with the slow clock behind them 6 to 8 us, 1862 to 1873. Rival F (the square's bank, not the fetch, makes the first one): the wait at 356 us stays, and only 3 to 4 us go.

> The same with the two HANDOVER edits (fetch:32 ahead of the block loads, the convolution weights' DMA one step earlier): another 6.8 us less, as those edits brought in the kernel with the load in the middle (1904.4 to 1897.6); 1861 to 1872.

> From the kernel with fetch and load in the middle and both HANDOVER edits, three words more: in HANDOVER the three block loads go behind R1:14 and u0:18 stands just ahead of u1:18; in BOUND u0:2 goes behind th1:-3, because ACT stood there 3.4 us for a block that was still landing, ahead of the tanh. Theory A3: R of pair 14 isn't late, and the waits of key products for ACT's tanh at 350, 778 and 1225 us (1.66, 1.69, 1.71) and for the square at 357 us (1.60) go: 5 to 7 us, 1863 to 1866. Rival: the pieces behind them take over and less than 2 us go.

In the changed kernel the two waits in HANDOVER have a root of the same kind, a DMA that goes out too late. At 356.85 a key product waited for a square on VectorE, but VectorE had stood 4.34 us for xs, whose fetch was behind three block loads. At 394.94 one waited for ACT's tanh, behind a scaling that waited 3.74 us for weights. e7 shortened the first to 1.31 and removed the second, though a new one of 1.35 for the tanh came at 349. Its forecast of 1862 to 1873 was missed, since it took e5 to be the repair that it wasn't. The 6.8 us to e5 are the 6 to 8 that were expected, but the two intervals overlap. On e14 the same edits were worth 4.7, clear of the noise, where 6.8 were expected. In e16, whose time fell in its range, the tanh waits at 350, 778 and 1225 us are gone. The one for the square was expected to go and didn't; it grew from 1.60 to 3.26 us. R isn't late there any more, but VectorE stood 4.79 us for xs, whose fetch now goes out right behind the three loads (e16's timeline):

```profile
362.29 3.34 PE L807 MATMUL pk<-y,wk_s 128*128 128x512 f32 x4 [3.26 <-DVE h L821]
```

e16 is 0.31% faster than the kernel before (0.22 to 0.40%), some 6 us: that is what the new lists are worth with these repairs, most of them to the places of DMAs. The old lists weren't given the same care, and loads issued from another engine's queue weren't tried.

## Why the prediction was wrong

The step that failed is "ORDER: 21 slots with almost no gap", taken at −0.5 with bounds of −2 and +2. It priced products, rc and cp by TensorE's distances and didn't price SP's queue: no word on where y3's store, the load, the fetch, W and R stand to each other, nor on in1 and in0, though the prediction itself says that positions change on all five queues. It measured +66 (eight times 5.9 to 7.3 us of waiting and 1.5 to 2.7 of slow clock), and one wait of 1.86 in the last stretch. The round trip of 8.4 us was taken as fixed, though the trace of before already had the part from W to R at 2.3 us without a store ahead and at 3.5 to 4.9 with one. The bounds were drawn from the gaps that the old list had, and an old list's gaps say nothing about what a new order can open. The rival on the slower side looked for the danger in the square's bank, where there was next to none. The clause that new stalls of over 3 us in ORDER would refute the lists was met.

Two sums of the prediction don't hold, though nothing hangs on them: 1871.1 less 1780 leaves 91 us of gaps, not 85, and the 2.6 us for R come from a formula that the page gives for DMAs issued by GpSimd, while R goes out from SP (the prediction went on with the trace's 3.44).

The other steps, from the changed kernel's trace:

| step | forecast, us | found, us |
|---|---|---|
| squares | 0 | 0 by the times (0.7 and 0.15 in two pairs of runs), 0.37 in one slot |
| FILL | +1.8; first key product at 77, pk10 near 82 | about +1.7 (estimate below); 76.40 and 81.06 |
| FIRST | 0; slots of 19.87 | about +1; slots of 19.93, one of 20.30 |
| HANDOVER, dated stalls | 4.85 to 2.85 | 6.00 (2.76 and 3.24), slow clock on top |
| BOUND, first | 4.31 to 1.31 | 2.81 (0.82 + 0.65 + 1.34) |
| BOUND, second | 2.50 to 1.00 | 1.29 |
| END | 5.05 to 2.55 | 7.23 |

FILL's size was right, its place wasn't. By the prediction's own count (time less TensorE's work done) the offset at 100 us is 67.5, where it was 66.5. This run had started its first token transposes 0.7 us earlier (33.89 against 34.61), which makes FILL's part an estimated +1.7. But by 77 us the count is already 66.7 against 65.7: the loss lies ahead of the first key product. pk10 came when it was forecast, and TensorE didn't wait for it, as the products ahead of it ran at half speed (three in the 3.8 us from 76.40). In FIRST the spare of 0.14 us held but for one slot, where a key product waited 0.17 us for the square; at 20.30 us that slot is above the 20.0 that the prediction had set as the sign of being wrong on the squares. It isn't so that each list has the same operations as the old one: that holds for ORDER, FIRST and BOUND, and for all lists together, but HANDOVER has 37 words fewer and END 40 more. What these two cost isn't compared like with like.

In BOUND the named stalls went as argued. In their place came waits for ACT's tanh: two, of 1.34 and 1.29, behind a u that waits some 3 us for a block, and one, of 0.82, behind a norm that waits for POOL's factors. END went the other way. VectorE's long stand at cp came as forecast (5.44 us at 1717.26), and TensorE lost nothing by it. But pm waits 1.86 us, about as before (1.90), though the list puts it earlier, and the 1.54 for an e and the 1.81 for the gate's se are new:

```profile
1787.51 0.38 PE L559 MATMUL pm<-mv,gmat 128*128 128x1 f32 x2 [1.86 <-DVE mv L556]
1805.11 1.10 PE L876 MATMUL m<-v,u 128*128 128x512 f32 x2 [1.81 <-DVE se L619]
```

What in the new END list makes se late wasn't tried.

## What to carry to other kernels

When an order is rewritten, write out the DMA queue's new list first: which DMA waits for a buffer, what is behind it, and how long the shortest road from a buffer's last reader to its next one has become. A list that fits the engines' durations to the tenth has no room for a transfer of 5 us that isn't in it. And of two delays with one root, the repair of either alone shows only a part of the gain (here half to two thirds), so a half-successful experiment isn't yet a refuted theory.

## What the hardware showed unexpectedly

A write of four rows of 1 KB took 2.3 us from issue to the read behind it where no large transfer was near, 3.5 to 4.9 us just behind a 1 MB store, and 5.7 us beside a 1 MB load and a 512 KB fetch. TensorE's clock after an idle time wasn't a matter of its length alone, nor was 3.4 us a floor: in e5 two of seven att products behind idle times of about 2.5 us ran at half speed (2.05 us at 1047.18, after 2.54) and five at full speed (1.13 at 583.31, after 2.56); in e1 and e5 no product behind an idle time below 2.0 us was slow in ORDER.
